# How the gate projection reads x: in read-out order on TensorE, or contiguously with the order made by a copy on ScalarE

## The chip, the cores and the metric

The kernel runs on one core of one Trainium2 chip. The metric is the device time of the whole program in microseconds, the median of several runs; lower is better. The engines are TensorE (PE; its weight loads are listed apart as PEld), VectorE (DVE), ScalarE (ACT), GpSimd (POOL), and SyncE (SP), which only issues DMAs here. [...]

## What is computed

The input x has 32 sequences of 256 steps with 256 channels. It passes through a conditioned state-space block and then through a transformer of two layers; the result is added to x. All arithmetic is in float32, apart from a few masks. Of the reference, the first block matters here:

```python
xr, gate = jnp.split(x @ W_in.T, 2, axis=-1)          # 512 + 512 channels
xr = xr + t_emb[:, None, :]
xc = silu(causal depthwise conv of 4 taps over xr)
xn = layernorm(xc) * ln_g + ln_b
Bm, Cm, dt = jnp.split(xn @ W_xproj.T, 3, axis=-1)    # 16 states
...
h = clip(h * ad + bd * xt, -10, 10); yt = ct . h      # a scan over the 256 steps
y = ys + D * xn
return y * jax.nn.silu(gate) @ W_out.T
```

Then each of two layers does windowed attention with eight heads, rotary positions and a shift of half the channels by one step, and a gated feed-forward of width 682. The gate of the first block, `silu(gate)`, is what the change touches.

## The kernel before

The 32 sequences are worked on in four groups of eight (`GB = 8`). For each group the scan block (`group_scan`) runs over eight chunks of 32 steps (`CH = 32`). The scan of group 0 runs alone; after that, the attention and feed-forward of group g (`blocks`) are issued side by side with the scan of group g+1: `side_by_side` takes one piece of the scan after every so many pieces of the layers. The layers of the last group have no scan beside them.

Inside `group_scan`, an agenda sets the order. `at(s, what, ...)` puts a function into step s, and the steps are issued in order; a step is about one step of the recurrence. For chunk c, with `s0 = 32 * c`:

- `load_x` (L340), at s0 - 43, loads x of the chunk into `xg`, which has two buffers: 128 channels on the partitions, then two halves of channels, eight sequences, 32 steps.
- `project` (L322) multiplies x by W_in for one slice of 128 output channels, two matmuls of 256 columns for the two halves of the input channels, into half a PSUM bank. Slices 0 to 3 are xr, and slices 4 to 7 are the gate. The xr slices are at s0 - 40 and on, the gate's at s0 + 13, 16, 17 and 18. In the trace a matmul of float32 is two records, so one projection is four.
- The xr slices go on to `conv_in`, `conv_taps` and `conv_out` (L360 to L390), the normalisation (L418 to L466) and the figures of the recurrence. Rows of the normalised input go out to DRAM and come back repeated over the partitions (`load_rows`, L547); in group 0, half of the rows are spread by TensorE instead (L555). `scale_row` (L566, ScalarE) multiplies a row by beta, two steps ahead, and `step` (L573, VectorE) does one step of the recurrence for all states. `read_out` (L585, TensorE) sums over the states.
- `gate_th` (L617) is at one step after the gate's projection: ScalarE takes the tanh of half the projection, out of the bank. `gate_out` (L622), one step later: VectorE makes `(tanh + 1) * projection`, which is twice the silu, reading the bank again, and writes slice ch of `sg`. `sg` has one buffer.
- `gated`, `out_turn` and `out_gate` (L630 to L656) add the skip, turn the result, and multiply it by `sg` (L652). The last `out_gate` of a chunk is at s0 + 40, which is step 8 of the next chunk. `project_y`, `copy_y` (L672) and `put_y` bring the result out; `copy_y` is a ScalarE copy from a bank to SBUF that changes the order of columns.

`read_out` puts the steps on the partitions in the order q, i, b (a step is 4 i + q, b is the sequence), with the sequence innermost. What meets it at L652 must have its columns in the same order. Before the change TensorE makes that order for the gate: the moving operand is x read in steps, so that the columns of the bank come out in read-out order.

```python
x = ck[c]["xg"][:, k]
if ch >= NC_:
    x = x.rearrange("p b (i q) -> p q i b", q=NQ)
nc.tensor.matmul(ps, w_in_sb[:, k, ch * P : (ch + 1) * P], x, ...)
```

In `xg` the steps of one sequence lie together, so neighbouring columns of the gate's matmul are 32 elements apart, while the xr slices read 256 elements in a row.

All uses of PSUM in the main program take their bank from one pool of eight (`ps_w`), in turn: a new bank waits until the one taken eight turns ago has been read for the last time. [...]The scheduler of the framework keeps the order of issue for the most part and may exchange neighbours.

The layers' operations that come up below are: `project_qkv` (L781), the rotary part on VectorE and GpSimd (L794 to L814), the turn of queries and keys (L820), the scores with their mask (L979, L986) and exponent (L995), sums and values (L1005 to L1031), the feed-forward's normalisation (L1064 to L1091), its wide matmuls (L1111), and its narrow ones (L1140).

## Time and profile before

| what | value |
|---|---|
| median of 3 runs | 4182.01 us (4180.69 to 4185.67) |
| the profiled execution, its time | 4183.47 us |
| the profiled execution, its span | 4181.7 us |
| mean granted TensorE clock | 0.966 |
| group 0's scan alone, then first layers start | 0 to 465 us |
| layers of groups 0 to 2 beside a scan | 465 to 3480 us |
| layers of group 3, no scan beside | 3480 to 4182 us |
| L330, all projections: matmul records | 1024 (128 gate and 128 xr projections of 4) |
| L619 tanh of the gate, from the bank | 128 times, 382 ns |
| L625 gate product, VectorE | 128 times, 416 ns |
| L382 tanh of the convolution, from SBUF | 128 times, 414 ns |
| L387 product of the convolution, all in SBUF | 128 times, 485 ns |
| L672 copy from a bank into strided SBUF | 64 times, 604 ns |

The last five rows are the groups of the profile with all shapes kept apart. In a group's row the numbers after the bar are the busy time of the group in us and the mean length of one instruction in ns; after the second bar stands the time for which the engine was idle just ahead of these instructions, and what ended most of it. Matmuls overlap in the pipeline, so a record's length is more than its distance from the next; where a distance is meant, it is taken from the starts in the order of time. A row of that order merges neighbours of one line: start, length, engine, line, operation, the tiles, the form and the number.

A row of the stretches has the stretch's bounds and length, then for each engine its busy time and number of instructions, then the granted clock, the share of the DMA engines and GB/s.

### The profile page before, as it was taken

Reading aid. Unit: us, or ns where it says so; the run is one execution under the profiler, and the core shown is the slowest. Engines: PE = TensorE matmul, PEld = TensorE weight load, DVE = VectorE, ACT = ScalarE, POOL = GpSimd, SP = SyncE. Lnnn points to the kernel's source line nnn. Section 1 sums busy time; section 2 is a strip of 40 time slices with the busy share of each in tenths; the row PEclk is TensorE's granted clock in tenths of the full one; section 3 lists DMA queues with packets and bytes.
Section 4 is the critical chain, followed back from the end, with each engine's and each line's share of the span. In section 5 each row is a group of like instructions: output and inputs, shape, how many; then the busy total and the mean of one; then the engine's idle time right before and its main releaser. Section 6 shows DMA issues by size and latency. Waiting matters only on the chain. (4 is left out here: it accounts for less than half of the span.)

```text
span 4181.7 us, 51837 instructions
## 1 busy us (share of the span) xinstructions
PE 3874.3 (93%) x18236; PEld 2002.1 (48%) x18236; DVE 2619.7 (63%) x4986; ACT 1742.8 (42%) x3217; POOL 1708.1 (41%) x1749
## 2 busy tenths in 40 slices
PE   6999899899988999899998999989998899999999
PEld 3333355444544455444455445544454545654653
DVE  5888467677766456766867636776776644434443
ACT  2555344444444334444544424444444533322331
POOL 3443265225543156423654136522454315513531
PEclk9999899999999999999999999999999999999999
DMA  3444213444335212344434421344433521000000
GB/s 123 121 124 119 58 44 95 113 117 112 91 87 139 81 43 77 111 110 111 116 86 114 121 65 44 81 126 111 118 91 84 142 78 37 3 19 22 1 11 31
DMA packets 257345, 353.09 MB, mean 84 GB/s; under 512 B 160867, under 2 KB 170420, under 8 KB 254900
## 3 DMA queue, kind: packets, MB, share of 16 engines
q1 hardware_dynamic: 172624, 337.67, 29.0%
q10 hardware_dynamic: 84452, 12.01, 1.8%
q8 instruction: 147, 2.41, 0.2%
q14 instruction: 122, 1.00, 0.1%
HBM read 314.49 MB, written 33.55 MB: 83 GB/s over the span
## 5 line engine op out<-in xcount | busy, mean ns | idle before, releaser
L573 DVE CUSTOM_DVE_ANT_0 h<-h,xrep,lim 128x512 f32<-128x512 f32 x1024 | 908.1, 887 | 94.8 <-PE y L585 36.0
L566 ACT ACTIVATE xrep<-xrep,beta 128x512 f32<-128x512 f32 x896 | 608.6, 716 | 793.3 <-DMA xrep<-xnd 732.8
L781 PE MATMUL ps_qkv<-wqkv_sb,res 128*128 128x512 f32 x1536 | 740.5, 621 | 28.4 <-ACT qT L825 6.6
L805 POOL TENSOR_TENSOR rot<-rot,swp 128x512 f32<-128x512 f32 x256 | 329.2, 1286 | 653.3 <-DVE swp L802 603.3
L781 PEld LDWEIGHTS ps_qkv<-wqkv_sb,res 128*128 128x128 f32 x1536 | 286.6, 196 | 381.9 <-issue 309.0
L813 POOL TENSOR_TENSOR rn<-ss,neg_half 128x8 f32<-128x8 f32 x256 | 437.4, 1708 | 21.6 <-DVE ss L811 9.7
L797 DVE TENSOR_TENSOR rot<-ps_qkv,rc_sb 128x512 f32<-128x512 f32 x256 | 175.6, 686 | 375.6 <-ACT sq L794 375.4
L330 PE MATMUL ps_in<-xg,w_in_sb 128*128 128x256 f32 x1024 | 398.4, 523 | 6.5 <-ACT pT L995 3.4
L1140 PE MATMUL po_f<-ag,w_sb 128*128 128x512 f32 (+1 forms) x768 | 356.0, 612 | 18.5 <-DVE ag L1121 18.5
L585 PE MATMUL y<-h,ly 128*32 128x512 f32 x2048 | 354.0, 639 | 11.3 <-DVE h L573 10.1
L1111 PE MATMUL pa<-hT,w_sb 128*128 128x512 f32 (+1 forms) x896 | 363.0, 595 | 0.0
L1121 DVE SCALAR_TENSOR_TENSOR ag<-pa,b_sb,gl 128x512 f32<-128x512 f32 x192 | 143.5, 747 | 317.9 <-PE pa L1111 166.2
L1111 PE MATMUL pg<-hT,w_sb 128*128 128x512 f32 x640 | 309.4, 606 | 0.0
L330 PEld LDWEIGHTS ps_in<-xg,w_in_sb 128*128 128x128 f32 x1024 | 194.1, 204 | 206.5 <-issue 125.2
L814 POOL TENSOR_TENSOR rot<-rot,rn 128x512 f32<-128x512 f32 x256 | 280.3, 1095 | 19.0
L377 DVE SCALAR_TENSOR_TENSOR acc<-xr,wc_sb,acc 128x256 f32<-128x256 f32 x384 | 199.2, 523 | 116.7 <-POOL acc L366 114.2
L1074 POOL TENSOR_TENSOR rstd<-ve,neg_half 128x1 f32<-128x1 f32 x128 | 75.8, 592 | 476.6 <-DVE ve L1072 466.1
L995 ACT ACTIVATE pT<-sc 128x512 f32<-128x512 f32 x384 | 206.3, 592 | 127.3 <-PE sc L986 113.7
L831 PE MATMUL ps_wo<-oT,wo_sb 128*128 128x256 f32 x1024 | 237.3, 385 | 0.0
L1140 PEld LDWEIGHTS po_f<-ag,w_sb 128*128 128x128 f32 (+1 forms) x768 | 135.1, 190 | 203.3 <-issue 138.7
L794 ACT ACTIVATE sq<-ps_qkv 128x512 f32<-128x512 f32 x256 | 148.8, 593 | 195.9 <-PE ps_qkv L781 148.1
L1111 PEld LDWEIGHTS pa<-hT,w_sb 128*128 128x128 f32 (+1 forms) x896 | 135.6, 170 | 189.3 <-issue 175.7
(151 smaller groups left out, 5592.9 us busy)
## 6 DMA issues: line engine op xcount, KB each, us to landing
xrep<-xnd SPq DMA_DIRECT2D x448, 512.0 KB
xnd<-xn SPq DMA_DIRECT2D x64, 256.0 KB
wqkv_sb<-in_wqkv_dram SPq DMA_DIRECT2D x8, 1536.0 KB
xd<-xnd SPq DMA_DIRECT2D x192, 64.0 KB
w_sb<-in_w_dram SPq DMA_DIRECT2D x8, 1364.0 KB
xg<-in_xT_dram SPq DMA_DIRECT2D x64, 128.0 KB
ys<-yo ACTq DMA_DIRECT2D x64, 128.0 KB
res<-ys SPq DMA_DIRECT2D x32, 256.0 KB
```

The lines of the kernel that those rows point to most:

```text
L330: nc.tensor.matmul(ps, w_in_sb[:, k, ch * P : (ch + 1) * P], x, start=(k == 0), stop=(k == KM - 1),)
L566: nc.scalar.activation(bx, ck[c].pop(("bx", t), bx), AF.Copy, scale=ck[c]["beta"][:, t : t + 1])
L573: nc.vector._custom_dve(TENSOR_ADD_SAT, out=h_new, in0=state["h"], in1=bx, s0=ck[c]["lim"][:, 0, t : t + 1], s1=ck[c]["lim"][:, 1, t : t + 1],
L585: nc.tensor.matmul(ck[c]["y", hb][32 * q : 32 * q + 32, :], ly[hb % 2][:, 32 * t : 32 * t + 32], ck[c].pop(("h", hb * TB + t)), start=(i = ...
L781: nc.tensor.matmul(ps, res[b // 2][:, k, b % 2, t0 : t0 + W], wqkv_sb[:, k, a * DI : (a + 1) * DI], start=(k == 0), stop=(k == KM - 1),)
L805: nc.gpsimd.tensor_add(rot, rot, swp)
L813: nc.gpsimd.tensor_tensor(rn, ss, neg_half, ALU.pow)
L814: nc.gpsimd.tensor_mul(rot, rot, bc(rn, 2, DH))
L831: nc.tensor.matmul(po[:, d], wo_sb[:, c, d * P : (d + 1) * P], oT[:, c, :], start=(c == 0), stop=(c == NC_ - 1),)
L995: nc.scalar.activation(p, banks[r], AF.Exp)
L1111: nc.tensor.matmul(ps[0:n, :], self.w1[:, k, half_ * HID + o : half_ * HID + o + n], self.h[j][:, k].rearrange("p b t -> p (b t)"), start= ...
L1140: nc.tensor.matmul(self.po[d], self.w2[r0 : r0 + n, m, d * P : (d + 1) * P], self.ag[m][r0 : r0 + n, :], start=(m == 0), stop=(m == len(MC ...
```

## The change

The gate's projection reads x as the xr projection does, 256 elements in a row, and its bank comes out in the order b, i, q. A new helper, `reorder`, is called at the head of `gate_th`: a ScalarE copy reads the bank in order and writes the slice of `sg` with the columns moved to read-out order, in steps of 64 elements for neighbouring q. The tanh then reads that slice of `sg` in SBUF instead of the bank, and the product on VectorE reads the tanh and the slice and writes over the slice. The allocation of `sg` moves from `gate_out` to `gate_th`, one step earlier. The places in the agenda are not changed.

```diff
+        def reorder(out, ps):
+
+            nc.scalar.copy(
+                out.rearrange("p (q i b) -> p b i q", q=NQ, b=GB),
+                ps.rearrange("p (b i q) -> p b i q", q=NQ, b=GB),
+            )
+
...
             def project(c, ch):
 
-
                 ps = bank(ps_w, "w", "ps_in")[:, 0 : GB * CH]
                 for k in range(KM):
-                    x = ck[c]["xg"][:, k]
-                    if ch >= NC_:
-                        x = x.rearrange("p b (i q) -> p q i b", q=NQ)
                     nc.tensor.matmul(
                         ps,
                         w_in_sb[:, k, ch * P : (ch + 1) * P],
-                        x,
+                        ck[c]["xg"][:, k],
                         start=(k == 0),
                         stop=(k == KM - 1),
                     )
...
             def gate_th(c, ch):
-                th = sp.tile([P, GB * CH], FP, tag="th", name="th_g", bufs=2)
-                nc.scalar.activation(th, ck[c]["ps", NC_ + ch], AF.Tanh, scale=0.5)
-                ck[c]["th"] = th
-
-            def gate_out(c, ch):
                 if ch == 0:
                     ck[c]["sg"] = sp.tile([P, NC_, GB * CH], FP, tag="sg", name="sg")
+                sg = ck[c]["sg"][:, ch]
+                reorder(sg, ck[c].pop(("ps", NC_ + ch)))
+                th = sp.tile([P, GB * CH], FP, tag="th", name="th_g", bufs=2)
+                nc.scalar.activation(th, sg, AF.Tanh, scale=0.5)
+                ck[c]["th"] = th
+
+            def gate_out(c, ch):
+                sg = ck[c]["sg"][:, ch]
                 nc.vector.scalar_tensor_tensor(
-                    ck[c]["sg"][:, ch], ck[c].pop("th"), 1.0, ck[c].pop(("ps", NC_ + ch)),
-                    ALU.add, ALU.mult,
+                    sg, ck[c].pop("th"), 1.0, sg, ALU.add, ALU.mult
                 )
```

## The prediction

> **What bounds the kernel now.** I read the whole-span rows of the page first, then the busy time by stage, then the instructions of the line that the change touches, then TensorE's order of time around single gate projections, and last the waits.

> ```profile
> PE 3874.3 (93%) x18236; PEld 2002.1 (48%) x18236; DVE 2619.7 (63%) x4986; ACT 1742.8 (42%) x3217; POOL 1708.1 (41%) x1749
> ...
> L330 PE MATMUL ps_in<-xg,w_in_sb 128*128 128x256 f32 x1024 | 398.4, 523 | 6.5 <-ACT pT L995 3.4
> ```

> TensorE is busy for 93% of the span, and the next engine for 63%. The span is 4181.7 us; 4181.7 - 3874.3 leaves TensorE 307 us idle, so time taken off TensorE comes off the span as far as no wait swallows it. The second row is the line that changes: 10% of TensorE's time, with a mean of 523 ns for 256 columns.

> ```profile
> 300.00:400.00 100.00, 94.84 (x358) 35.59 (x358) 87.76 (x166) 56.46 (x105) 40.38 (x47) 0.95 0.47 121
> ...
> sum 1686.00, PE 1523.89 PEld 868.51 DVE 1160.14 ACT 766.37 POOL 948.83; mean PE 253.98 PEld 144.75 DVE 193.36 ACT 127.73 POOL 158.14
> ...
> sum 1329.00, PE 1269.56 PEld 607.42 DVE 807.68 ACT 537.47 POOL 329.66; mean PE 211.59 PEld 101.24 DVE 134.61 ACT 89.58 POOL 54.94
> ```

> Busy time in stretches. The first row is the scan of group 0, which runs alone: TensorE 95% and VectorE 88%, two engines close to the bound. The second is the sum of the six attention stretches (465 to 3280 us, a scan beside each): TensorE 90%, VectorE 69%. The third is the six feed-forward stretches: TensorE 96%, VectorE 61%. Counting the tanh L619 in the same stretches places the 128 gate projections: 32 in group 0, 38 in attention, 58 in feed-forward.

> ```profile
> L330 PE MATMUL ps_in<-xg,w_in_sb x1024: 379/621/797, 37.2 to 3372.1; 128*128 128x256 f32 x171
> ...
> 876.10 1.94 PE L330 MATMUL ps_in<-xg,w_in_sb 128*128 128x256 f32 x4
> 877.86 1.90 PE L1111 MATMUL pg<-hT,w_sb 128*128 128x512 f32 x4
> ...
> 900.48 1.03 PE L330 MATMUL ps_in<-xg,w_in_sb 128*128 128x256 f32 x4
> 901.43 1.06 PE L585 MATMUL y<-h,ly 128*32 128x512 f32 x8
> 904.69 1.03 PE L330 MATMUL ps_in<-xg,w_in_sb 128*128 128x256 f32 x4
> 905.55 1.88 PE L1111 MATMUL pg<-hT,w_sb 128*128 128x512 f32 x4
> ...
> 145.21 3.81 PE L330 MATMUL ps_in<-xg,w_in_sb 128*128 128x256 f32 x8
> 148.95 1.13 PE L555 MATMUL bx<-xq,rep_w 32*128 32x512 f32 x4
> ```

> The line has two populations, 379 ns at the least and 621 at the median. A projection is four records. The one at 876.10 feeds the gate (the tanh and L625 follow it) and holds TensorE for 1.76 us until the next group starts; those at 900.48 and 904.69 feed the convolution (L360 follows) and hold it for 0.95 and 0.86 us. At 145.21 two gate projections stand back to back: 3.74 us, 1.87 each. Weights, shapes and types are alike; only the order in which x is read differs.

> [...] the trace has tanh at 414 ns from SBUF (L382) and 382 from PSUM (L619), 32 more. [...] This page shows no loss of clock through dense work: the feed-forward stretches have 0.97 to 0.99. I charge nothing for a denser TensorE.

> **The change part by part.**

> 1. *Contiguous reads.* A gate projection becomes the contiguous kind. It goes from 1.76 to 1.87 us down to 0.86 to 0.95: 1.87 - 0.95 = 0.92, 1.76 - 0.86 = 0.90, and the merged rows of one projection, 1.94 and 1.03, differ by 0.91. I take 0.92, and 128 x 0.92 = 118 us of TensorE. How much stays in each stage: feed-forward, 58 x 0.92 = 53 us; TensorE is 96% busy, its stalls (2 to 3 us at L1140 and L1089) are few, I keep 0.9: 48. Attention, 38 x 0.92 = 35 us; 10% idle, and stalls behind VectorE and GpSimd (L979 behind L802, L820 behind L814, L1089 behind L1072) follow the gates by 3 to 55 us, where an earlier TensorE partly waits longer; I keep 0.7: 24. Group 0, 32 x 0.92 = 29 us; a chunk takes 48.5 us (the gate pair recurs at 145.2, 193.5 and 242.0) with 43 us of VectorE, so most of the 3.7 us that TensorE saves per chunk becomes waiting for L573; I keep 0.4: 12. Sum 84 us.

> 2. *The added ScalarE copy.* 128 copies, PSUM read in order, SBUF written in steps. The nearest row is L672, also 256 elements out of a bank into strided SBUF: 604 ns. 128 x 0.604 = 77 us; ScalarE goes from 42% to 44%. It hides in ScalarE's idle time (L566 alone waits 733 us for its DMA). Its step is 256 bytes where L672's is 128: below I take the 382 ns of a plain pass out of the bank, above 1.2 us, twice L672, since the trace has no such step. I take 0.604. Queued behind it on ScalarE are L566 (VectorE's steps wait), L995 and L794 (TensorE and VectorE wait).

> 3. *Tanh from SBUF* and its new wait on the copy: 32 ns more each, 4 us of ScalarE. The wait on ScalarE's own result is at most the 2.7/6 = 0.45 us that L672 shows, and nothing where another operation stands between (the built order has one between in about half of the cases in group 0). Together tanh ends 0.604 + 0.03 to 0.45 later against its matmul, which ends 0.92 earlier: 0.28 earlier to 0.16 later. VectorE's L625, which heads its queue with L573 behind it, now waits 120 us for tanh; that stays about as it is. Cost 0.

> 4. *L625 from SBUF in place*: up to 69 ns, 128 x 0.069 = 9 us of VectorE, 2 of them in group 0. Elsewhere VectorE's 31 to 39% of idle time hides it; in group 0 it is on the path. Cost 2; without the cover, 9.

> 5. *Banks.* A gate's bank is now freed by the copy and no longer by tanh and L625. Waits of TensorE put down to L625 or L619 sum to under 15 us; I credit 2, bounds 0 and 10.

> 6. *sg written earlier, by another engine.* sg has one buffer, so the first copy of a chunk must wait for L652 of the chunk before, planned six steps earlier (step 40 of one chunk is step 8 of the next, the copy at 14). ScalarE runs two steps ahead of VectorE, so it is free by then. Cost 0; if not, ScalarE stands still with L566 behind it.

> 7. *Order.* In the built program TensorE's order is the same in groups 1 to 3; in group 0 one or two L585 per chunk change places with L330 or L661. SyncE's loads of xg shift by one L547 and stand 15 us ahead of their use (issued 1072.7, read 1087.7); no wait on them is in TensorE's list. They also wait for the last gate projection (108 us on SyncE in all), which now ends sooner, with the row loads L547 behind them. Cost 0.

> Sum: -84 + 2 - 2 = -84. The profiled execution took 4183.5 us (span 4181.7): 4183.5 - 84 = 4099.5. The runs shown have a median 1.5 us lower, so 4098.

> **The rivals.**

> *A: the gain stays in feed-forward only.* Attention and group 0 are paced by VectorE and GpSimd chains; for it speak the 88% in group 0 and the L805 and L813 chains that L820 waits for; against it the 90% of TensorE in attention, with long runs without a stall. 58 x 0.92 x 0.85 = 45: 4183.5 - 45 - 1.5 = 4137. Chance 20%.

> *B: nearly everything is kept*, since VectorE and GpSimd also wait for TensorE and move up with it, and the banks help. 118 + 4: 4060. Chance 10%.

> *C: slower, by ScalarE's queue.* The place is the copy ahead of tanh, L566 and L995. It decides when copy plus own wait plus 32 ns exceed the 0.92 us saved, that is from a copy of 0.44 to 0.89 us, depending on the own wait, and when L625's lateness blocks L573 on the path. At 1.2 us: 1.2 + 0.45 + 0.03 - 0.92 = 0.76 us late at each of the 66 places where L625 already waits, 50 us of VectorE; if TensorE then loses its 118 us to waits for h, rows and softmax, and 0.4 of the 50 shows, +20: 4202. Chance 5%.

> *D: it doesn't do what it says*: the slow records come from something other than the order of the reads. 4182, within the noise. Against it: the two kinds stand 25 us apart at the same clock. Chance 3%.

> **How the numbers follow.** The likeliest case has 62%: 4098, its own range 4075 to 4122. The range 4066 to 4142 takes in that case, most of A and half of B. A measurement of this kernel tells 0.2%, some 8 us, from no change. Faster 0.62 + 0.20 + 0.10 = 0.92, same 0.03 (D), slower 0.05 (C).

> **What would show it.** Step 1: all of L330's matmuls near 384 ns and its busy time near 398 - 118 = 280 us; TensorE's total near 3756. Step 2: the new copy's row near 604 ns x128. Step 3 and 4: tanh 414, L625 towards 485, their waits near 120 us. Stage shares: the six feed-forward stretches together shorter by about 48 us, attention by 24, group 0 by 12. Wrong if TensorE's idle time grows by over 70 us (A), if copies take over 0.9 us (C), or if L330 stays at 621 (D).

## The result, and the profile after

| what | before | after |
|---|---|---|
| median of the runs, us | 4183.84 (4180.69 to 4186.25) | 4156.98 (4152.3 to 4163.51) |
| ratio after to before, 95% interval | | 0.994 (0.9926 to 0.9954) |
| span of the profiled execution, us | 4181.7 | 4150.5 |
| TensorE busy; idle (span less busy), us | 3874.3; 307.4 | 3797.3; 353.2 |
| mean granted TensorE clock | 0.966 | 0.959 |

The change makes the kernel faster by 0.6%, about 27 us, where 84 were forecast. The spans of the two profiled executions differ by 31.2 us, and that is the figure which the accounts below divide.

The whole-span row and the row of the changed line, from the page of the kernel after:

```profile
PE 3797.3 (91%) x18236; PEld 2008.9 (48%) x18236; DVE 2627.6 (63%) x4986; ACT 1810.9 (44%) x3345; POOL 1699.9 (41%) x1749
...
L333 PE MATMUL ps_in<-xg,w_in_sb 128*128 128x256 f32 x1024 | 291.1, 414 | 12.8 <-issue 4.5
```

and from the view of one tile, with the shortest, the median and the longest duration in ns:

```profile
L333 PE MATMUL ps_in<-xg,w_in_sb x1024: 379/379/796, 37.3 to 3341.5; 128*128 128x256 f32 x171
...
L307 ACT COPY sg<-ps_in x128: 616/640/698, 95.2 to 3345.1; 128x256 f32<-128x256 f32 x128
```

The line of the projection (L330 before, L333 now) has lost its slow population: the median is the minimum. Its busy time fell from 398.4 to 291.1, by 107.3 us. But TensorE as a whole fell by 77.0 only, and its idle time grew by 45.8. So 107.3 = 31.2 kept + 45.8 more idle + 30.3 that other TensorE work now takes longer. The last term is the one to stop at: nothing was added to TensorE.

The new copy and the two operations behind it, groups of the kernel after with the shapes kept apart:

```profile
L307 ACT COPY sg<-ps_in 128x256 f32<-128x256 f32 x128 | 81.7, 638 | 21.0 <-PE ps_in L333 17.2 <-ACT yo L677 3.1 <-PE ps_wo L836 0.4
L631 DVE SCALAR_TENSOR_TENSOR sg<-th_g,sg 128x256 f32<-128x256 f32 x128 | 68.5, 535 | 103.9 <-ACT th_g L626 103.1
L626 ACT ACTIVATE th_g<-sg 128x256 f32<-128x256 f32 x128 | 53.1, 415 | 2.8
```

The copy takes 638 ns and waits for little but its bank (17.2 of 21.0 us); the tanh has 2.8 us of idle time ahead of it in all; the product takes 535 ns in the mean where it took 416.

**By stage.** I cut both traces at the same events: the first `ps_qkv` matmul of each layer and the first `pa` matmul of its feed-forward. These stretches differ from those in the prediction: there, the feed-forward stretches began 25 to 36 us earlier and ended 36 to 60 us later, and so took in attention at both ends. Times in us; "L330" is its busy time in the stretches, "other" the rest of TensorE's busy time, "half clock" what the clock records of the trace take off (length times one less the granted clock; the records are 1.00 or 0.50; the pieces at 0.50 last 3.4 to 13.7 us after the change, and before it one lasts 30.7). It is an upper bound of what half clock cost: in 51 of the 285 us at half clock before, TensorE stood anyway.

| stretch | length before, after | change | L330 | other | idle | half clock |
|---|---|---|---|---|---|---|
| group 0 alone | 475.3, 478.1 | +2.8 | -28.8 | +14.7 | +16.8 | +7.3 |
| attention, layer 0 (3) | 976.5, 974.1 | -2.4 | -17.9 | +2.1 | +13.4 | +1.3 |
| feed-forward, layer 0 (3) | 458.0, 448.5 | -9.5 | -10.9 | +1.5 | -0.1 | +1.7 |
| attention, layer 1 (3) | 1146.2, 1129.0 | -17.2 | -38.9 | +9.9 | +11.7 | +13.7 |
| feed-forward, layer 1 (3) | 387.6, 383.7 | -3.9 | -10.9 | +3.4 | +3.6 | +3.4 |
| layers of group 3 | 738.1, 737.1 | -1.0 | 0 | -1.5 | +0.4 | +0.1 |

"Change" is the sum of the three columns that follow. Laid over the clock records, "other" has two sources. In the four stretches of groups 0 to 2 that have a scan beside them, TensorE's other work grows by 16.9 us: it is busy 36.4 us more at half clock and 19.4 us less at full clock, as it would be if the same matmuls moved to half speed and took twice as long. In group 0 alone only 4.5 of the 14.7 us lie at half clock. There most of the rest is the read-out (L585 before, L588 now), busy for 10.9 us more at full clock: the same 512 records come in 113 bursts instead of 104, and at full clock a burst of two records takes 1.04 us (at 330.42 after the change), one of eight 1.06 (at 307.21). In the trace of the kernel after, three stretches in group 0:

```profile
301.70:311.70 10.00, 7.23 (x35) 2.89 (x34) 7.08 (x11) 7.78 (x16) 3.67 (x3) 1.00 0.47 130
311.70:321.90 10.20, 8.12 (x20) 2.80 (x18) 7.67 (x18) 4.68 (x10) 2.91 (x3) 0.50 0.42 111
321.90:332.00 10.10, 10.10 (x43) 3.66 (x40) 9.15 (x22) 3.31 (x6) 5.59 (x12) 1.00 0.29 80
```

and TensorE there, in order of time:

```profile
307.21 1.06 PE L588 MATMUL y<-h,ly 128*32 128x512 f32 x8
310.88 0.63 PE L643 MATMUL tz<-ident,xd 128*128 128x128 f32 x4 [2.60 <-DVE xd L637]
311.44 1.70 PE L588 MATMUL y<-h,ly 128*32 128x512 f32 x2
315.22 1.14 PE L485 MATMUL ps_st<-rhs,sel 128*128 128x96 f32 x4 [2.08 <-DVE rhs L484]
316.29 2.08 PE L558 MATMUL bx<-xq,rep_w 32*128 32x512 f32 x4
318.30 2.08 PE L333 MATMUL ps_in<-xg,w_in_sb 128*128 128x256 f32 x4
```

The third figure from the right in the stretches' rows is the clock: 1.00, 0.50, 1.00. TensorE had stood for 2.60 us; from 311.70 the clock is half for 10.2 us, and a contiguous projection (at 318.30) takes 2.08 us instead of 1.03. The wait is paid, and then paid a second time.

### The profile page after: what moved, and what is told of

Its sections match the earlier page's. It is cut to its first block, busy times and chain, and to the rows that moved or that the text cites. A ratio compares the mean times of both kernels' runs of the same rounds, so it can differ in the third digit from the quotient of the medians.

```text
span 4150.5 us, 51929 instructions
## 1 busy us (share of the span) xinstructions
PE 3797.3 (91%) x18236; PEld 2008.9 (48%) x18236; DVE 2627.6 (63%) x4986; ACT 1810.9 (44%) x3345; POOL 1699.9 (41%) x1749
## 5 line engine op out<-in xcount | busy, mean ns | idle before, releaser
L576 DVE CUSTOM_DVE_ANT_0 h<-h,xrep,lim 128x512 f32<-128x512 f32 x1024 | 894.7, 874 | 82.5 <-PE y L588 23.3
L786 PE MATMUL ps_qkv<-wqkv_sb,res 128*128 128x512 f32 x1536 | 750.2, 628 | 32.5 <-ACT oT L1036 8.2
L818 POOL TENSOR_TENSOR rn<-ss,neg_half 128x8 f32<-128x8 f32 x256 | 436.7, 1706 | 23.3 <-DVE ss L816 11.7
L802 DVE TENSOR_TENSOR rot<-ps_qkv,rc_sb 128x512 f32<-128x512 f32 x256 | 175.7, 686 | 393.3 <-ACT sq L799 392.9
L588 PE MATMUL y<-h,ly 128*32 128x512 f32 x2048 | 362.0, 631 | 14.3 <-DVE h L576 13.1
L333 PE MATMUL ps_in<-xg,w_in_sb 128*128 128x256 f32 x1024 | 291.1, 414 | 12.8 <-issue 4.5
L333 PEld LDWEIGHTS ps_in<-xg,w_in_sb 128*128 128x128 f32 x1024 | 191.0, 201 | 156.0 <-issue 71.9
L991 PE MATMUL sc<-qT,kT 64*128 64x128 f32 (+1 forms) x2048 | 227.1, 352 | 1.9 <-ACT kT L830 1.8
```

Source lines behind the costliest of these rows:

```text
L333: nc.tensor.matmul(ps, w_in_sb[:, k, ch * P : (ch + 1) * P], ck[c]["xg"][:, k], start=(k == 0), stop=(k == KM - 1),)
L576: nc.vector._custom_dve(TENSOR_ADD_SAT, out=h_new, in0=state["h"], in1=bx, s0=ck[c]["lim"][:, 0, t : t + 1], s1=ck[c]["lim"][:, 1, t : t + 1],
L588: nc.tensor.matmul(ck[c]["y", hb][32 * q : 32 * q + 32, :], ly[hb % 2][:, 32 * t : 32 * t + 32], ck[c].pop(("h", hb * TB + t)), start=(i = ...
L786: nc.tensor.matmul(ps, res[b // 2][:, k, b % 2, t0 : t0 + W], wqkv_sb[:, k, a * DI : (a + 1) * DI], start=(k == 0), stop=(k == KM - 1),)
L818: nc.gpsimd.tensor_tensor(rn, ss, neg_half, ALU.pow)
L991: nc.tensor.matmul(banks[r][:, i, :], kT[rows, i0 + i, kw * W : (kw + 1) * W], qT[rows, i0 + i, kw * W :], start=False, stop=(i == n - 1),)
```

## The experiments

Two theories to begin with. **Pace**: other engines' chains set the time in group 0 and attention, so that TensorE's saving turns into waiting. **Queue**: the saving is real, and the copy in ScalarE's queue gives it back. All ratios are to the kernel before, with 95% intervals, from runs beside it.

| run | median us | ratio (95%) | span | TensorE idle | clock | lost to half clock |
|---|---|---|---|---|---|---|
| before | | 1 | 4181.7 | 307 | 0.966 | 142 |
| after | 4156.98 | 0.994 (0.9926 to 0.9954) | 4150.5 | 353 | 0.959 | 170 |
| e1_matmul_only | 4143.31 | 0.991 (0.9889 to 0.9931) | 4141.9 | 349 | 0.957 | 178 |
| e2_copy_only | 4200.38 | 1.0045 (1.0028 to 1.0063) | 4202.6 | 330 | 0.967 | 139 |
| e3_x_once | 4144.91 | 0.9911 (0.9892 to 0.993) | 4147.2 | 363 | 0.960 | 166 |
| e4_group0_before | 4145.49 | 0.9914 (0.9894 to 0.9934) | 4144.2 | 343 | 0.962 | 157 |
| e5_rows4 | 4125.91 | 0.9881 (0.9858 to 0.9903) | 4130.3 | 354 | 0.960 | 165 |
| e6_more_pe | 4252.67 | 1.0181 (1.0154 to 1.0207) | 4256.4 | 305 | 0.973 | 115 |
| e7_half_gate | 4130.39 | 0.9894 (0.9868 to 0.9921) | 4125.6 | 363 | 0.957 | 177 |
| e8_before_rows4 | 4169.47 | 0.9988 (0.9974 to 1.0002) | 4170.4 | 297 | 0.965 | 146 |
| e9_x_once_no_clamp | 4155.66 | 0.9942 (0.9925 to 0.996) | 4160.0 | 361 | 0.957 | 179 |
| e10_before_no_clamp | 4185.98 | 1.0016 (1.0006 to 1.0026) | 4184.1 | 308 | 0.963 | 155 |
| e11_group0_strided | 4137.51 | 0.9899 (0.9875 to 0.9923) | 4138.1 | 336 | 0.964 | 149 |
| e12_rows_early | 4130.55 | 0.9889 (0.9869 to 0.9909) | 4125.8 | 360 | 0.964 | 149 |
| e13_before_rows_early | 4171.78 | 0.9982 (0.9971 to 0.9992) | 4175.7 | 306 | 0.966 | 142 |
| e14_x_once_no_norm | 4045.3 | 0.9675 (0.9649 to 0.97) | 4044.6 | 289 | 0.968 | 129 |
| e15_before_no_norm | 4070.04 | 0.9747 (0.9718 to 0.9777) | 4061.3 | 234 | 0.977 | 93 |
| e16_norm_first | 4023.96 | 0.9624 (0.9591 to 0.9657) | 4018.5 | 278 | 0.971 | 117 |
| e17_before_norm_first | 4073.23 | 0.9747 (0.972 to 0.9774) | 4055.8 | 236 | 0.979 | 85 |

Idle is the span less TensorE's busy time, and the last column is the span times one less the mean clock; both are of the one profiled execution.

### The two halves of the change, each alone

`e1_matmul_only` reads contiguously and has no copy: tanh and product read the bank as before, and the gate's columns stay in the order b, i, q.

```diff
-                    if ch >= NC_:
-                        x = x.rearrange("p b (i q) -> p q i b", q=NQ)
```

> The gate's matmuls read x in a row, and tanh and product take the bank as before: no copy. The gate's columns then stand in the order b, i, q where read-out order is wanted, so this computes another function. Theory 'pace' (the chains of VectorE and GpSimd set the time, so most of TensorE's saving turns into waiting whatever the gate costs on ScalarE): close to the changed kernel, 4150 +- 10 us. Theory 'queue' (the saving is worth about the forecast 84 us, and the copy in ScalarE's queue gives two thirds of it back): 4105 +- 15 us. In both TensorE's time on the projections falls from 398 to about 290 us.

`e2_copy_only` keeps the read in steps and adds the copy, the tanh from SBUF and the product in place.

```diff
+                reorder(sg, ck[c].pop(("ps", NC_ + ch)))
-                nc.scalar.activation(th, ck[c]["ps", NC_ + ch], AF.Tanh, scale=0.5)
+                nc.scalar.activation(th, sg, AF.Tanh, scale=0.5)
...
-                    ck[c]["sg"][:, ch], ck[c].pop("th"), 1.0, ck[c].pop(("ps", NC_ + ch)),
-                    ALU.add, ALU.mult,
+                    sg, ck[c].pop("th"), 1.0, sg, ALU.add, ALU.mult
```

> The gate's matmuls read x in steps as in the kernel before, and the copy, the tanh from SBUF and the product in place are added. The columns are permuted twice, so this computes another function. Theory 'pace': the copy hides in ScalarE's idle time, 4184 +- 8 us. Theory 'queue': the copy costs what it gives back in the changed kernel, about 50 us: 4235 +- 15 us.

The saving alone is worth 0.9%, some 38 us of the 105 that e1's projections lost (398.4 to 293.4). The copy alone costs 0.45%, some 19 us; inside the change it is the difference of 0.994 and 0.991, about 12 us, which the intervals allow to be 2 or 23. So mostly *pace*, with a real but small part of *queue*.

### The order made elsewhere, and group 0 left as it was

`e3_x_once` puts x itself into read-out order, once a chunk: two ScalarE copies of 0.70 us from SBUF to SBUF, 13 steps ahead of the chunk, in place of four copies out of the bank beside the gate. The gate's matmul reads `xo`; tanh and product are those of the kernel before.

```diff
+            def order_x(c):
+                xo = sp.tile([P, KM, GB * CH], FP, tag="xo", name="xo")
+                for k in range(KM):
+                    nc.scalar.copy(
+                        xo[:, k].rearrange("p (q i b) -> p b i q", q=NQ, b=GB),
+                        ck[c]["xg"][:, k].rearrange("p b (i q) -> p b i q", q=NQ),
+                    )
+                ck[c]["xo"] = xo
...
+                at(s0 - 13, order_x, c)
```

> x of a chunk is put in read-out order once, by two ScalarE copies of 256 elements from SBUF to SBUF, 27 steps ahead of the gate, in place of four copies out of the banks; xg and the ordered x have one buffer each, as much room as xg had. Tanh and product take the bank as before. Theory 'pace': about 4150 us, as the changed kernel. Theory 'queue': nothing is added between projection, tanh and product, and half as many copies lie elsewhere in the queue: 4110 +- 20 us, the fastest so far that computes the reference's function.

`e4_group0_before` is the changed kernel whose group 0 does as before (`if ch >= NC_ and alone`, and the old tanh and product there).

> Group 0, whose scan runs alone, has the projection, tanh and product of the kernel before; groups 1 to 3 those of the changed kernel. In the changed kernel the eighth chunk of group 0 starts 10 to 14 us late, and the first layers start 2.8 us late. If that lateness comes from the copy in group 0, it goes away: the first layers start at 475 +- 3 us and the whole takes 4150 +- 6 us. If the change gains in group 0 and other things lose, this is slower than the changed kernel: 4165 us.

e3 equals e1 (0.9911 and 0.991): the order can be had at no cost that can be told when its copies aren't beside the gate. e4 is 0.26 points faster than the change itself, with intervals that just overlap: group 0 keeps nothing, and seems to have paid for its 32 copies.

### TensorE heavier and lighter: what is its time worth?

`e6_more_pe` issues the gate's matmul for k = 0 twice in the kernel before, in steps: 109 us more by its rows. `e7_half_gate` is e1 with half of the gate's matmuls: 59 us less than e1 by its rows.

```diff
-                for k in range(KM):
+                ks = (0, 0, 1) if ch >= NC_ else (0, 1)
+                for n, k in enumerate(ks):
```

> The kernel before, with the gate's matmul over the first half of the input channels issued twice into the same sum: the gate counts that half twice, so another function is computed; 256 more strided records of 447 ns, 114 us of TensorE. If TensorE paces the kernel before, +90 to +114 us. If it has as little weight upwards as the 36 us for 118 downwards, +35 us. A knee between the two directions would give about +70 us and more.

> Contiguous reads without the copy, and the gate's matmul over the second half of the input channels alone: the gate leaves out half of its sum and stands in another order, so another function is computed. 256 contiguous records fewer, 55 us of TensorE less than with contiguous reads alone (4143 us). At the rate of 36 us for 118 it saves another 17: 4126 us. If the rest of the saving lies in places where TensorE no longer counts, under 10: 4138 us. If the saving grows once a threshold is passed, 40 or more: 4100 us.

Upward, a microsecond of TensorE costs 0.7 of one (1.81% is 76 us, for the 109 of the rows). Downward, the first 105 bring about 38 (0.36), and the next 59 bring 0.16 points, 7 us, which the intervals don't tell from nothing. The kernel before stands at a knee. Group 0 shows it best. Its row before, after, and in e6:

```profile
0.00:475.30 475.30, 409.49 (x1437) 157.46 (x1437) 358.75 (x704) 220.69 (x402) 161.02 (x223) 0.93 0.44 116
```

```profile
0.00:478.10 478.10, 395.47 (x1437) 161.91 (x1437) 365.24 (x704) 235.25 (x434) 156.79 (x223) 0.91 0.45 116
```

```profile
0.00:477.30 477.30, 414.76 (x1501) 165.37 (x1501) 359.79 (x704) 219.80 (x402) 158.66 (x223) 0.97 0.44 116
```

With 64 matmul records more, 25.4 us of L330 in this stretch (104.2 before, 129.7 in e6), group 0 lasts 2.0 us longer, and its clock rises from 0.93 to 0.97: TensorE had the time, and it lost less to half clock by using it. With 28.8 us less it lasts no shorter, and its clock falls to 0.91.

### Which chain paces attention? Rows, VectorE, or the norm

The trace names three suspects. ScalarE stands for repeated rows from DRAM (L566, 733 us), with the squares (L794) and VectorE's rotary products behind them; VectorE carries the sums of squares; GpSimd ends the chain with an addition, a power and a product (L805 to L814).

**Rows.** `e5_rows4` is e3 with four buffers of rows, the room taken from `zT` (the out gate writes over `sg`); `e8_before_rows4` does that to the kernel before; e12 and e13 also issue each load seven steps ahead, not five.

```diff
-        xp = ctx.enter_context(tc.tile_pool(name="xp", bufs=3, reuse_waits="tile"))
+        xp = ctx.enter_context(tc.tile_pool(name="xp", bufs=4, reuse_waits="tile"))
...
-                        at(s0 + t - 5, load_rows, c, t)
+                        at(s0 + t - 7, load_rows, c, t)
```

> The version that orders x once, with a fourth buffer for the repeated rows xrep; its room comes from writing the gated output over sg in place of zT. ScalarE stands for about 640 to 690 us in groups 1 to 3 waiting for rows, with the squares, copies and exponents of the layers behind it. Theory 'rows' (these waits set the pace in the attention stretches and so swallow TensorE's saving): the waits shrink to under half and the time falls to 4110 +- 15 us. Theory 'chains' (the pace is the rotary and softmax chain over VectorE, GpSimd and ScalarE itself): no change, 4145 +- 8 us.

> The kernel before with the fourth buffer for the rows alone, made in the same way. Theory 'rows' with TensorE as the next bound: it gains less than it does on top of the ordered x, 4165 +- 10 us against 4179. Theory 'chains': no change, 4179 +- 8 us.

> The kernel with x ordered once a chunk and four buffers of repeated rows, each transfer of rows issued seven scan steps ahead and not five. ScalarE stands 599 us for these rows in the version it is made from, and the squares that VectorE's rotary products wait for are queued behind. 'Rows' (this chain from a late transfer over ScalarE and VectorE takes the saving in attention): ScalarE's wait for the rows falls below 400 us, VectorE's wait for the squares with it, and the ratio is 0.979 to 0.985. 'Not rows': 0.987 to 0.990, whatever these waits do.

> The kernel before with four buffers of repeated rows and the same transfers seven steps ahead. 'Rows' with TensorE nearer its limit here: 0.993 to 0.997, a smaller gain than the lighter kernel has of the same edit. 'Not rows': 0.998 to 1.000.

ScalarE's longest wait before, and in e5 and e12 (total, times, longest):

```profile
ACT xrep L566 <- DMA xrep<-xnd: 732.8, 309, 8.4
```

```profile
ACT xrep L575 <- DMA xrep<-xnd: 599.0, 266, 8.3
```

```profile
ACT xrep L575 <- DMA xrep<-xnd: 600.2, 260, 8.5
```

The fourth buffer takes 145 us off this wait (744 in e3, 599 in e5; 733 before, 588 in e8). It brings 0.3 points in e5 over e3, and 0.12 in e8, where the interval reaches past 1. Issuing earlier didn't shorten the wait (600 in e12, 621 in e13), so e12 and e13 test less than they were meant to, and neither time can be told from e5's and e8's. What can be said is that a fifth of the wait is worth about 12 us in the lighter kernel and 5 in the kernel before; the intervals allow nothing, and some 25 us.

**VectorE.** e9 (on e3) and e10 (on the kernel before) leave out the line that bounds the sum of squares: 117 us off VectorE, 0.46 off every chain.

```diff
-            nc.vector.tensor_scalar_max(ss, ss, 1e-24)
```

> The kernel that orders x once a chunk, without the line that bounds the sum of squares below before the reciprocal root (a guard for a zero norm; it leaves that guard out and nothing else). It takes 256 VectorE instructions of 0.46 us, 117 us, off VectorE and the same 0.46 us off each rotary chain, and nothing off TensorE. Compare with 0.991 for the same kernel with that line. 'Chains' (once TensorE is lighter, the rotary work over VectorE, GpSimd and ScalarE sets the pace of attention, so TensorE's saving stood as waiting for it): 0.981 to 0.986, and TensorE's idle time falls by 25 us or more with its own work unchanged. 'No chain' (the missing gain is not with VectorE; it is in half clock and in other waits): 0.988 to 0.991.

> The kernel before, without that same line (it leaves the guard for a zero norm out and nothing else). 'Chains', with TensorE and the rotary chains about balanced in the kernel before: it gains less than the lighter kernel does, 0.995 to 0.998, since TensorE then binds. 'No chain': 0.998 to 1.000. If it gains as much as the lighter kernel, then both kernels are bound by the chains to the same degree, and the balance I read from the runs with more and with less TensorE work is wrong.

e10's row of the page:

```profile
PE 3876.1 (93%) x18236; PEld 2007.6 (48%) x18236; DVE 2528.7 (60%) x4730; ACT 1743.7 (42%) x3217; POOL 1712.1 (41%) x1749
```

VectorE is 91 us lighter (the scan's steps, L573, take 16 us more), and neither kernel gains; both are a little slower, outside the numbers of both theories. VectorE's load isn't the pace. The slowness I can only place: in layer 1's attention e10 is 12.6 us longer than the kernel before, and the clock records take 18.8 us more there. Why the half clock falls more often isn't shown.

**The norm.** e14 (on e3) and e15 (on the kernel before) leave the power out, and with it the last product's wait for the sum of squares.

```diff
-            rn = aw.tile([P, HEADS], FP, tag="rn", name="rn")
-            nc.gpsimd.tensor_tensor(rn, ss, neg_half, ALU.pow)
-            nc.gpsimd.tensor_mul(rot, rot, bc(rn, 2, DH))
+            nc.gpsimd.tensor_mul(rot, rot, bc(neg_half, 2, DH))
```

> The kernel that orders x once a chunk, with queries and keys scaled by a constant and not by the norm: the power on GpSimd (256 times 1.71 us, 437 us) is left out, and the last product of the rotary chain waits for neither the power nor the sum of squares. TensorE's work is unchanged. 'GpSimd's end of the rotary chain sets the pace of attention once TensorE is lighter': TensorE's stall for the turned queries and keys falls, attention of groups 0 to 2 gets shorter by 30 us or more, and the ratio is 0.976 to 0.984. 'No single chain' (many small stalls with different causes, and half clock after them): 0.986 to 0.991, within 20 us of 0.991 for the same kernel with the norm.

> The kernel before with the same part left out. If GpSimd's chain paces only the lighter kernel, this gains less than the lighter kernel does: 0.993 to 0.998. If it gains as much (both by a similar share), the chain costs both kernels the same and does not explain where the saved TensorE time went. 'No single chain': 0.996 to 1.000.

This is the first thing that paces: 2.5% in the kernel before, and 0.9675 / 0.9911 = 0.976, 2.4%, in the lighter one. But it paces both alike. The reads with x ordered once are worth 0.9675 / 0.9747 = 0.993 without the chain and 0.991 with it (about 0.4 points either way for such a quotient). So the norm's chain isn't where the saving went. Both gains are larger than any figure I had put down; of the cases written down for e15, the one that came is the middle one, the same gain in both.

**The same with nothing left out.** In e16 (on e5) and e17 (on the kernel before) the sum of squares comes ahead of the rotary products, so that the power runs beside them, and VectorE does the addition.

```diff
+            ss = aw.tile([P, HEADS], FP, tag="ss", name="ss")
+            nc.vector.tensor_reduce(
+                ss, sq.rearrange("p (h d) -> p h d", h=HEADS), AX.X, ALU.add
+            )
+            nc.vector.tensor_scalar_max(ss, ss, 1e-24)
+            rn = aw.tile([P, HEADS], FP, tag="rn", name="rn")
+            nc.gpsimd.tensor_tensor(rn, ss, neg_half, ALU.pow)
             rot = ap_.tile([P, HEADS, DH], FP, tag="rot", name="rot", bufs=4)
...
-            nc.gpsimd.tensor_add(rot, rot, swp)
+            nc.vector.tensor_add(rot, rot, swp)
...
```

> The version with x ordered once a chunk and four buffers of rows (0.988), with the norm of queries and keys moved ahead of the rotary products: VectorE sums the squares first, so that GpSimd's power (1.71 us) runs beside VectorE's products, and VectorE adds the two products (0.69 us) where GpSimd did in 1.29. The function is the reference's. The chain from the squares to the last product gets shorter, from about 5.5 us to about 4, an estimate from the durations in the page. 'The norm's chain paces attention': 0.965 to 0.980. 'VectorE and the bank take it back' (banks of queries and keys are read out 0.9 us later, VectorE has 160 us more): 0.985 to 0.995.

> The kernel before with the same edit of the rotary chain and nothing else. If the chain costs both kernels the same, as leaving the power out has shown (2.5% here, 2.4% in the lighter kernel), the gain is that of e16 over its own base, within 0.4 points: 0.976 to 0.992. If it is below 0.2%, the gain of leaving out the power came from GpSimd's time and not from the length of the chain.

TensorE's turn of queries and keys, before and in e17; the idle time stands behind the second bar:

```profile
L820 PE MATMUL tr_qk<-ident,rot 128*128 128x128 f32 x1024 | 143.1, 280 | 51.2 <-POOL rot L814 23.6 <-DVE swp L802 13.0 <-POOL res L771 11.5
```

```profile
L820 PE MATMUL tr_qk<-ident,rot 128*128 128x128 f32 x1024 | 136.6, 274 | 29.3 <-POOL rot L814 11.4 <-DVE swp L810 9.4 <-POOL res L771 6.6
```

and e17's whole-span row:

```profile
PE 3819.9 (94%) x18236; PEld 1987.3 (49%) x18236; DVE 2673.7 (66%) x5242; ACT 1744.6 (43%) x3217; POOL 1375.6 (34%) x1493
```

A shorter chain with the power still in it brings what leaving the power out brings, 0.9747 both times, though VectorE has 54 us more. e17's span is 125.9 us shorter: 71.5 less idle and 54.4 less TensorE busy time with the same matmuls, at a clock of 0.979 instead of 0.966 (the profiled execution is e17's fastest; by the medians it is 106 us).

The two pairs do not separate the length of the chain from GpSimd's load: e15 and e17 both take work off GpSimd as well (1708 us before, 1277 in e15, 1376 in e17). For the length speaks that GpSimd, in the kernel before, stood idle ahead of its additions, mostly for VectorE's last rotary product:

```profile
L805 POOL TENSOR_TENSOR rot<-rot,swp 128x512 f32<-128x512 f32 x256 | 329.2, 1286 | 653.3 <-DVE swp L802 603.3
```

And e16, with the ordered x and the four buffers besides, is the fastest of all: 0.9624, about 157 us under the kernel before and 3.2 points under the change. Over e17 that is 0.987, as e5 over e8 is 0.989.

### Group 0 once more

`e11_group0_strided` is e5 with group 0 reading in steps and no `order_x` there; its chunks of x take turns in the buffers of x and of the ordered x. With a single buffer of x in group 0 (e11_best) the instructions wait for each other in a circle, and there is no time to compare.

> x ordered once a chunk in groups 1 to 3, group 0 reading with the step as before (its chunks of x take turns in the two buffers of x and of the ordered x), the out gate writing over the gate's tile, four buffers of repeated rows. 'Pace': group 0 is bound by VectorE and keeps nothing of the saving, so leaving it as it was costs nothing: 0.986 to 0.989, against 0.988 with group 0 changed too. 'Queue' (the saving in group 0 is real): 0.990 to 0.992.

0.9899 against e5's 0.9881, with intervals that overlap: leaving group 0 alone costs nothing that can be told, and saves nothing either. The run doesn't tell the two theories apart.

## Why the prediction was wrong

The direction held, and the mechanism of step 1 held for each projection. The size failed: 27 us and not 84, with 4157 outside the range of 4066 to 4142.

1. *Contiguous reads: the retention terms failed.* The saving on TensorE was mis-sized little (107 us by the rows for 118). What failed are the shares to be kept, 0.9, 0.7 and 0.4, and that no term of the sum stands for the clock: "I charge nothing for a denser TensorE" looked at the wrong side. Measured in the stretches above: feed-forward keeps 13.4 of 21.8 us (0.61), attention 19.6 of 56.8 (0.35), group 0 nothing of 28.8. The prediction also misplaced the projections, since its stretches took in attention: by the tanh L619, 24 and not 58 gate projections lie in feed-forward, 72 and not 38 in attention. That matters little: with these counts and the same shares its sum would have been 78. Three things took the rest. TensorE waits 46 us more, spread over many places: in layer 0's attention no stall grew by more than about 6 us. In group 0 the read-out, in shorter bursts, counts 11 us more as busy. And the clock: I asked whether dense work lowers it; the trace of before had the answer to the opposite question in its mean of 0.966, 142 us of lost clock, already there beside 307 us of waits. Fewer matmuls meant more waits and so more half clock, 28 us more. Where TensorE was given more work, in e6, the loss fell by 27 with nearly the same idle time (305 us for 307): it matters how the waits lie (the last section).
2. *The copy*: 638 ns against 604 taken, hidden "in ScalarE's idle time" at a cost of nothing. Alone it cost 0.45%, 19 us; within the change about 12. Idle time by the sum wasn't cover at each place.
3. *Tanh*: 415 ns and 0.02 us of waits apiece, as said.
4. *The product from SBUF*: mean 535 for "towards 485", 15 us on VectorE for at most 9. The operation itself isn't slower, but a few take over 600 ns; in the view of its line, shortest, median, longest, and below it the same operation before:

```profile
L631 DVE SCALAR_TENSOR_TENSOR sg<-th_g,sg x128: 409/424/1519, 99.9 to 3346.2; 128x256 f32<-128x256 f32 x128
```

```profile
L625 DVE SCALAR_TENSOR_TENSOR sg<-th_g,ps_in x128: 403/420/423, 95.6 to 3373.9; 128x256 f32<-128x256 f32 x128
```

The prediction's 69 ns are the mean of L387, all in SBUF, less that of L625 (485 less 416). L387 has 359, 419 and 1490: that reading rested on a mean, and the medians are 419 and 420. Of L631's 128 operations, 28 overlap a GpSimd operation in the trace; 17 of these take over 600 ns, and none of the other 100 more than 427. With the operand still in the bank, 50 of L625's overlap one and none takes more than 423. One of the 17, 1.49 us at 307.93, runs beside L461 (307.54 to 309.13). L387 in the kernel before goes with L631: 82 of its 128 overlap a GpSimd operation, 17 of these take over 600 ns, and none of the other 46 more than 427. So in these three lines the operations of over 600 ns all lie beside a GpSimd operation, and L625, with its operand in the bank, has none; what lengthens them isn't shown.

5. *Banks*: no gain of the kind shows, and none was tested by itself.
6. *One buffer of sg*: as said; the copy's waits have no L657 among them.
7. *Order*: nothing seen against it.

**The rivals.** A, by its time of 4137, was nearer than the forecast, but its reason was half right: group 0 kept nothing, yet the gain didn't stay in feed-forward alone, which gave 13 of the 31 us; attention gave 20. Its sign, 70 us more idle time, came at 46, since I hadn't counted that half clock hides in busy time. C's place was real, but its price was 12 to 19 us, too little to outweigh the reads. B and D are out.

**What stays open.** No single wait takes the saving. The chain that paces attention costs the lighter kernel and the heavier one alike, so the loss of some two thirds without any copy (e1) is shown only as an account, waits and half clock by stage, not as a cause that could be taken away. What went ahead of half clock is read from the traces (the last section); no run varied the gaps by themselves. Whether the norm's chain pays by its length or by GpSimd's load isn't separated.

## What to carry to other kernels

An engine that is 93% busy isn't the bound by that number: test what its time is worth by adding work to it and by taking some away, since the two slopes (here 0.7 and 0.36, then next to nothing) say where the knee is. Read the clock beside the busy time: matmuls at half clock look like work (the contiguous projection counted 2.08 us as busy at 0.50 and 1.03 at 1.00). In these kernels the loss to half clock came to 0.36 to 0.51 of TensorE's idle time, so in the mean a wait came with a loss beyond its own length, but that is an average and no price for one wait: e6 and the kernel before have the same idle time and differ by 27 us in the loss. Before making a busy engine cheaper, look for the chain of other engines that it stands behind; the edit of the norm's chain alone was worth four times what the whole change was.

## What the hardware showed unexpectedly

| TensorE busy in the step | steps | half clock in the next |
|---|---|---|
| under 40% | 652 | 652 |
| 40 to 80% | 1947 | 291 |
| over 80% | 18582 | 6 |

In the kernel before alone the three rows are 35 of 35, 19 of 98 and 0 of 996, and after the change 47 of 47, 13 of 90 and 0 of 967. And half clock ended 930 times, each time after a step that was at least 80% busy. The step before the 10.2 us above was 24% busy. So here a gap of 2.60 us was enough to leave a step sparse. Between 40 and 80% the busy share alone does not decide (291 of 1947). Group 0 agrees: between 117 and 470 us the kernel before has five steps followed by half clock, 49 to 67% busy; after the change there are seven, the emptiest at 24%; in e6, none is under 59% and none is followed by half clock.

- *A small VectorE operation took longer with GpSimd beside it.* The bound on 8 sums of squares, 128x8, in the kernel before and in e17, where GpSimd's power waits for it and a GpSimd operation overlaps only 21 of the 256 (238 before):

```profile
L811 DVE TENSOR_SCALAR ss<-ss x256: 156/334/1029, 486.9 to 4011.6; 128x8 f32<-128x8 f32 x128
```

```profile
L800 DVE TENSOR_SCALAR ss<-ss x256: 151/160/1023, 473.0 to 3888.0; 128x8 f32<-128x8 f32 x128
```

The mean goes from 463 to 195 ns with nothing changed in the operation but its place. Those that overlap no GpSimd operation take 160 ns in both; the 238 that overlap one in the kernel before take 486 ns in the mean.
